# Seven half-width products in place of one 256-cubed product, in three steps of a PSUM bank, and four token sums moved to GpSimd

## The chip, the cores and the metric

The program runs on one core of a Trainium2 chip. The metric is the device time of one execution in microseconds (us). The kernel before took 820.01 us (median of 3 runs, 819.54 to 820.28).

## What is computed

4096 tokens of width 1024 are normalized. From the normalized tokens two branches start. One is a gate with a recurrence over the sequence; the other a feed-forward with three weight matrices, whose rows are then added into only eight rows of the output, because the top-2 expert indices (0 to 7) are used as row indices:

```python
g = sigmoid(einsum('btd,ed->bte', u, gate_w) + gate_b)
u_g = u * g
...
h = silu(xr @ w1.T)
h = silu(h @ w3.T)
h = h @ w2.T
...
out = out.at[indices_k[:, k]].add(gates[:, k:k + 1] * h)
...
x = x + s * silu(ffn)
```

So all tokens go through `w1` and `w3` (two 1024 x 1024 matrices, float32), only the first 1024 tokens through the gate matrix, and `w2` is applied after the sum over tokens, to eight rows.

## The kernel before

**Groups and halves.** The 4096 tokens are cut into four groups (`sb` 0 to 3) of 1024. For a group the product with `w1` is called `u`, with `w3` is called `m`, and with the gate matrix `g` (group 0 only). Each is a 1024-cubed product done by two levels of Strassen in Winograd's form. The first level leaves seven products of 512 cubed; one such product is one `Half` (L885), numbered `i` 1 to 7 and run in the order of L205. The second level leaves seven products of 256 cubed, one per step of a half (`step`, L919).

**One step.** `small` (L869) does a 256-cubed product with four matmuls of 128 weights columns and 256 moving columns. The profile has two rows for each float32 matmul, here called passes, so that a step is eight passes. A half keeps its sums in three PSUM banks: `X` (steps 0, 2, 4, 6), `Z` (steps 1, 5) and `Y` (step 3 alone). After each step the bank, as it then stands, is added on VectorE to a quarter of the half's result in SBUF (`first`, L904, and `more`, L912; for halves 1 and 5, which have nothing to add to, `first` is a copy on ScalarE). There are two `X` banks, two `Z` banks and one `Y` bank (L104 to L106).

**Order.** Every engine's instructions run in the order in which the program emits them (`Pinned`, L79). The emission follows "places": a half starts 7 places after the one before and does step n at its start S + 2n, so two halves interleave and one place is one step of TensorE. Around the end of a half (place S + 12) TensorE's order is: step 6 of this half, step 3 of the next half, step 0 of the one after it, which takes over this half's `X` bank. Work for other engines is entered with `at(place, ...)` (L186) and emitted when the place comes.

**Operands.** The sums of tokens within a half (`left_sums`, L846) are four GpSimd subtractions or additions of 128 x 512 into "quarters", tiles of 128 x 512 in SBUF; there are 18 (L125). They are emitted 8 places ahead of their step. The sums of tokens for the first level (`s1` to `s4`, L785 to L844, four 128 x 512 instructions each) run on the engine that `s_engine` (L779) names: GpSimd for `u` of groups 1 to 3, VectorE for `m`. In group 0 the weights' sums are made and kept in DRAM; groups 1 to 3 load them again with `load_kept` and `load_kept_sum` (L629, L635), issued on SyncE's queue 9 or 10 places ahead.

**What comes between.** In `m` of groups 1 and 2 the tokens of the next group are normalized (`norm`, L407) with VectorE instructions of 128 x 1024, one every 1.9 places. Halves 6 and 7 add two blocks on VectorE after each quarter (`whole`, L1005). The routing of a group (`route`, L439) is spread over the first halves of its `u`; its one-hot sums on VectorE wait for two sigmoids on ScalarE.

Of the kernel before, what the change touches and what calls it, by code (L numbers as in the profile page):

```python
# [10 lines left out]
F32 = mybir.dt.float32  # L11
# [3 lines left out]
ALU = mybir.AluOpType  # L15
AX = mybir.AxisListType
P = 128
Q = 256
# [4 lines left out]
def kernel(  # L23
# [55 lines left out]
    class Pinned:  # L79
# [15 lines left out]
    nc = tc.nc  # L95
    pe, dve, act, pool, sync = (
        Pinned(e) for e in (nc.tensor, nc.vector, nc.scalar, nc.gpsimd, nc.sync)
    )
# [7 lines left out]
    ps_y = ctx.enter_context(tc.tile_pool(name="ps_y", bufs=1, space=bass.MemoryType.PSUM))  # L106
# [15 lines left out]
            if self.uses == 0:  # L122
                self.home.append(self.tile)

    NB, NQ = 20, 18  # L125
    IDLE = 13
    blocks = deque(
        const.tile([P, 4, 2 * Q], F32, tag=f"b{i}", name=f"b{i}") for i in range(NB)
# [8 lines left out]
    def quarter(uses=1):  # L137
        return Held(quarters, uses)
# [47 lines left out]
    def at(place, f, *args):  # L186

        seq[0] += 1
        heapq.heappush(todo, (place, seq[0], f, args))
# [8 lines left out]
    def resume(p, g):  # L198
        step = next(g, None)
        if step is not None:  # L200
            at(p + step, resume, p + step, g)
# [14 lines left out]
    start = {}  # L216
# [301 lines left out]
    kept = {}  # L518
    op_t = {}
# [14 lines left out]
    def keep_quarter(name, i, j, o):  # L534
        d = dramp.tile([P, 2 * Q], F32, tag=f"{name}_{i}_{j}", name=f"{name}_{i}_{j}")
        sync.dma_start(d, o.tile)
        kept[name, i, j] = d
        o.drop()
# [177 lines left out]
    def first_w3():  # L716
# [48 lines left out]
    S_OF = {  # L765
        1: (0, 0),
        2: (0, 1),
        4: (1, 1),
        5: "s1",
        6: "s2",  # L770
        3: "s4",
        7: "s3",
    }
    left = {}
# [2 lines left out]
    A_AT = (1, 2, 4, 5)  # L777

    def s_engine(kind, sb):  # L779
        return pool if kind == "u" and sb > 0 else dve  # L780


    BANKS = {("u", 0): (0, 1), ("m", 0): (0,)}
# [1 line left out]
    def s1(kind, sb, n):  # L785
        eng = s_engine(kind, sb)
        a21, a22 = left[kind, sb, (1, 0)], left[kind, sb, (1, 1)]
        o = block(1 + n)
        if (kind, sb) in BANKS:
            yield from with_bank(o, a21, a22, (3, 0, 1, 2), op=ALU.add, of=BANKS[kind, sb])  # L790
        else:
            for q in (3, 0, 1, 2):
                eng.tensor_tensor(o[:, q], a21[:, q], a22[:, q], ALU.add)
                if q == 0:
                    yield 0.5
        a21.drop()
        a22.drop()
        left[kind, sb, "s1"] = o

    def s2(kind, sb, n):  # L800
        eng = s_engine(kind, sb)
        while (kind, sb, "s1") not in left:
            yield 0.25
        p, a11 = left[kind, sb, "s1"], left[kind, sb, (0, 0)]
        o = block(2 * n)
        if (kind, sb) in BANKS:
            yield from with_bank(o, p, a11, (2, 3, 0, 1), of=BANKS[kind, sb])
        else:
            for q in (2, 3, 0, 1):
                eng.tensor_tensor(o[:, q], p[:, q], a11[:, q], ALU.subtract)  # L810
                if q == 3:
                    yield 0.5
        p.drop()
        a11.drop()
        left[kind, sb, "s2"] = o

    def s4(kind, sb, n):

        eng = s_engine(kind, sb)
        while (kind, sb, "s2") not in left:  # L820
            yield 0.25
        o, a12 = left[kind, sb, "s2"], left[kind, sb, (0, 1)]
        if (kind, sb) == ("m", 0):
            yield from with_bank(o, o, a12, (2, 3, 0, 1), True, of=(0, 2))
        else:
            for q in (2, 3, 0, 1):
                eng.tensor_tensor(o[:, q], a12[:, q], o[:, q], ALU.subtract)
                yield 0.5
        a12.drop()
        left[kind, sb, "s4"] = o  # L830
# [35 lines left out]
                yield 2 * (A_AT[j + 1] - A_AT[j])  # L866


    def small(ps, A, B, start, stop, rows_first):  # L869

        for mt in range(2):
            for kt in range(2):
                w, m = (A, B) if rows_first else (B, A)
                pe.matmul(
                    ps[:, mt * Q : (mt + 1) * Q],
                    w[:, kt * Q + mt * P : kt * Q + (mt + 1) * P],
                    m[:, kt * Q : (kt + 1) * Q],
                    start=(start and mt == 0 and kt == 0),
                    stop=(stop and mt == 1 and kt == 1),
                    skip_group_check=True,  # L880
                )
# [3 lines left out]
    class Half:  # L885
# [30 lines left out]
        def whole(self, q):  # L916
            whole(self.kind, self.sb, self.i, q)

        def step(self, n):  # L919
            if n == 0:  # L920
                self.begin()
            A, t = self.A, self.t
            ts = [op_ts.get((self.kind, self.sb, self.i, j)) for j in range(4)]
            s = [left_q.get((self.src, self.sb, self.i, j)) for j in range(4)]

            def go(ps, a, b, start, stop):
                small(ps, a, b, start, stop, self.rows_first)

            if self.plain:

                q = ((0, 1, 2, 3) if self.i == 1 else (0, 3, 1, 2))[n // 2]
                ps = self.X if n // 2 % 2 == 0 else self.Z
                go(ps, A[:, q // 2 * 2 + n % 2], t[:, n % 2 * 2 + q % 2], n % 2 == 0, n % 2 == 1)
                if n % 2:
                    self.first(q, ps)
            elif n == 0:
                go(self.X, A[:, 0], t[:, 0], True, False)
                self.first(0, self.X)
            elif n == 1:
                go(self.Z, s[0].tile, ts[0].tile, True, False)  # L940
                self.first(3, self.Z)
                s[0].drop()
                ts[0].drop()
            elif n == 2:
                go(self.X, s[1].tile, ts[1].tile, False, False)
                self.first(1, self.X)
                s[1].drop()
                ts[1].drop()
            elif n == 3:
                Y = ps_y.tile([P, 2 * Q], F32, tag="Y", name=f"Y_{self.tag}")  # L950
                go(Y, A[:, 1], t[:, 2], True, True)
                if (self.kind, self.i) == ("g", 1):
                    at(Y_AT, self.more, 0, Y)
                else:
                    self.more(0, Y)
            elif n == 4:
                go(self.X, s[2].tile, ts[2].tile, False, False)
                self.more(3, self.X)
                s[2].drop()
                ts[2].drop()  # L960
            elif n == 5:
                go(self.Z, s[3].tile, t[:, 3], False, True)
                self.more(1, self.Z)
                s[3].drop()
            elif n == 6:
                go(self.X, A[:, 3], ts[3].tile, False, True)
                self.first(2, self.X)
                self.whole(2)
                ts[3].drop()
            if n == (7 if self.plain else 6):  # L970
                self.A.drop()
                t.drop()
# [265 lines left out]
    for kind, sb, i, plain in line:  # L1238
        h = Half(kind, sb, i, plain)
        halves.append(h)  # L1240
        S = start[kind, sb, i]
        n = 2 if sb == 0 and kind == "u" and i not in PLAIN_G else 1
        if kind != "g" and not plain:
            at(S + 2 - 8, left_sums, kind, sb, i, n)
        if kind != "g" and sb > 0:
            at(S - 10, load_kept, kind, sb, i)
            for j in range(4):
                at(S + 2 * T_AT[j] - 9, load_kept_sum, kind, sb, i, j)

    for sb in range(NS):  # L1250
        n = 2 if sb == 0 else 1
# [252 lines left out]
```

## Time and profile before

| | us |
|---|---|
| median of the runs | 820.01 |
| profiled execution: first to last instruction (span) | 817.9 |
| TensorE matmul busy in it | 810.6 (99%), 4085 passes |
| VectorE busy | 509.7 (62%) |
| GpSimd busy | 496.1 (61%) |
| ScalarE busy | 263.8 (32%) |
| granted TensorE clock | 1.000 |
| one half of groups 1 to 3 on TensorE | 12.09 |

The profiled execution has no time of its own listed apart from its span; the median of the runs lies 2.1 us above the span, which is what surrounds the first and last instruction. In the rows of the timeline a line is: start in us, duration in us, engine, source line, operation, output<-inputs by tile names (buffer numbers left out), shape, number of instructions, and in brackets how long the engine had been idle and what released it. PE is TensorE's matmuls, PEld its weight loads, DVE VectorE, ACT ScalarE, POOL GpSimd, SP SyncE. A row with x8 is eight instructions in a row; its duration is from the first one's start to the last one's end, and a pass has an end that lies beyond the start of the next, since passes are pipelined. All compute rows have line L89, the helper that records them, so groups are told apart by tiles: `b` are the 128 x 2048 blocks, `q` the quarters, `X_m`, `Y_u` and so on the PSUM banks of a half, `bc` the rows of means and scales for the normalization.

The busy share of each engine by stretch of groups 1 to 3 (`u` and `m` of each group) is:

| stretch, us | what | VectorE busy, us | GpSimd busy, us |
|---|---|---|---|
| 292.2 to 358.5 | most of group 1's `u` | 35.12 of 66.3 | 39.92 |
| 358.5 to 469.0 | group 1's `m`, start of group 2's `u` | 70.03 of 110.5 | 60.32 |
| 469.0 to 535.3 | group 2's `u` | 35.09 of 66.3 | 34.79 |
| 535.3 to 645.8 | group 2's `m`, start of group 3's `u` | 70.04 of 110.5 | 60.31 |

### The profile page before, as it was taken

Reading aid. Unit: us, or ns where it says so; the run is one execution under the profiler, and the core shown is the slowest. Engines: PE = TensorE matmul, PEld = TensorE weight load, DVE = VectorE, ACT = ScalarE, POOL = GpSimd, SP = SyncE. Lnnn points to the kernel's source line nnn. Section 1 sums busy time; section 2 is a strip of 40 time slices with the busy share of each in tenths; the row PEclk is TensorE's granted clock in tenths of the full one; section 3 lists DMA queues with packets and bytes.
Section 4 is the critical chain, followed back from the end, with each engine's and each line's share of the span. In section 5 each row is a group of like instructions: output and inputs, shape, how many; then the busy total and the mean of one; then the engine's idle time right before and its main releaser. Section 6 shows DMA issues by size and latency. Waiting matters only on the chain.

```text
span 817.9 us, 11299 instructions
## 1 busy us (share of the span) xinstructions
PE 810.6 (99%) x4085; PEld 696.5 (85%) x4085; DVE 509.7 (62%) x868; ACT 263.8 (32%) x458; POOL 496.1 (61%) x398
## 2 busy tenths in 40 slices
PE   8999999999999999999999999999999999999997
PEld 7888888888888878888888788888888788888885
DVE  6886598765588524764985235666983246667643
ACT  1245126877232237341022065421122021220111
POOL 2799896967999394744547453755448454465300
PEclk9999999999999999999999999999999999999999
DMA  9946619465978947629955875559666365555700
GB/s 338 421 175 232 230 47 357 171 246 160 411 267 309 345 174 293 241 103 385 376 179 210 332 279 190 187 206 426 242 244 257 104 219 203 196 180 195 283 14 2
DMA packets 55927, 192.88 MB, mean 236 GB/s; under 512 B 6480, under 2 KB 9792, under 8 KB 44224
## 3 DMA queue, kind: packets, MB, share of 16 engines
q1 hardware_dynamic: 55552, 191.61, 63.5%
q8 instruction: 33, 0.54, 0.3%
q10 hardware_dynamic: 320, 0.54, 0.2%
q14 instruction: 22, 0.18, 0.1%
HBM read 169.01 MB, written 39.87 MB: 255 GB/s over the span
## 4 chain that ended last, share of the span: by engine, by line
PE 98%; DMA 1%; DVE 0%; ACT 0%; issue 0%; SPq 0%
PE X_u L89 24%; PE X_m L89 24%; PE Z_u L89 12%; PE Z_m L89 12%; PE X_g L89 6%; PE Y_m L89 6%; PE Y_u L89 6%; PE Z_g L89 3%; PE acc L89 2%; PE plT L89 2%; PE Y_g L89 1%; DMA b<-in_x 1%; PE pp L89 0%; DVE bn L89 0%; PE accB L89 0%; PE ta L89 0%
## 5 line engine op out<-in xcount | busy, mean ns | idle before, releaser
L89 POOL TENSOR_TENSOR q<-b 128x512 f32<-128x512 f32 x154 | 203.0, 1331 | 193.7 <-PE X_m L89 48.0
L89 ACT ACTIVATE b<-b 128x512 f32<-128x512 f32 (+1 forms) x152 | 105.3, 696 | 298.1 <-DVE b L89 291.6
L89 POOL TENSOR_TENSOR q<-b,q 128x512 f32<-128x512 f32 x98 | 133.1, 1361 | 7.2 <-issue 4.0
L89 POOL TENSOR_TENSOR b<-b,b 128x512 f32<-128x512 f32 x72 | 92.9, 1310 | 48.5 <-PE X_u L89 33.7
L89 DVE TENSOR_TENSOR b<-b,b 128x512 f32<-128x512 f32 x120 | 109.2, 925 | 2.7
L89 PE MATMUL X_m<-q,q 128*128 128x256 f32 x448 | 105.9, 379 | 0.0
L89 PE MATMUL X_u<-q,q 128*128 128x256 f32 x432 | 102.4, 380 | 0.0
L89 DVE TENSOR_TENSOR b<-X_u,b 128x512 f32<-128x512 f32 x87 | 60.0, 690 | 57.8 <-PE X_u L89 57.1
L89 DVE TENSOR_TENSOR b<-X_m,b 128x512 f32<-128x512 f32 x88 | 60.4, 688 | 56.9 <-PE X_m L89 56.7
L89 PEld LDWEIGHTS X_m<-q,q 128*128 128x128 f32 x448 | 85.0, 190 | 12.4 <-issue 0.8
L89 POOL TENSOR_TENSOR q<-q,b 128x512 f32<-128x512 f32 x56 | 73.6, 1314 | 32.4 <-PE X_u L89 25.1
L89 PEld LDWEIGHTS X_u<-q,q 128*128 128x128 f32 x432 | 81.8, 190 | 12.2 <-issue 1.2
L89 DVE TENSOR_TENSOR b<-b,bc 128x1024 f32<-128x1024 f32 x56 | 67.8, 1211 | 0.1
L89 PE MATMUL X_u<-b,b 128*128 128x256 f32 x248 | 58.4, 380 | 0.0
L89 PE MATMUL Y_m<-b,b 128*128 128x256 f32 x224 | 53.1, 380 | 0.0
L89 PE MATMUL Z_m<-b,q 128*128 128x256 f32 x224 | 53.0, 380 | 0.0
L89 PE MATMUL X_m<-b,b 128*128 128x256 f32 x224 | 53.0, 379 | 0.0
L89 PE MATMUL Z_m<-q,q 128*128 128x256 f32 x224 | 52.9, 379 | 0.0
L89 PE MATMUL X_m<-q,b 128*128 128x256 f32 x224 | 52.9, 379 | 0.0
L89 PEld LDWEIGHTS X_u<-b,b 128*128 128x128 f32 x248 | 47.0, 190 | 6.7 <-DVE b L89 0.4
L89 DVE TENSOR_TENSOR b<-Z_u,b 128x512 f32<-128x512 f32 x47 | 32.4, 690 | 31.6 <-PE Z_u L89 30.7
L89 PE MATMUL Z_u<-q,q 128*128 128x256 f32 x216 | 51.1, 380 | 0.0
(182 smaller groups left out, 1171.6 us busy)
## 6 DMA issues: line engine op xcount, KB each, us to landing
q<-w SPq DMA_DIRECT2D x168, 256.0 KB, 4.5
b<-in_w SPq DMA_DIRECT2D x36, 1024.0 KB, 9.0
b<-w_T SPq DMA_DIRECT2D x24, 1024.0 KB, 6.3
b<-in_xT SPq DMA_DIRECT2D x15, 1024.0 KB, 12.9
w<-q SPq DMA_DIRECT2D x56, 256.0 KB, 7.4
b<-in_x SPq DMA_DIRECT2D x12, 1024.0 KB, 11.0
w_T<-b SPq DMA_DIRECT2D x8, 1024.0 KB, 4.4
b<-in_gw SPq DMA_DIRECT2D x6, 1024.0 KB, 14.0
```

Of the source, the lines that this page charges most:

```text
L89: r = f(*args, **kwargs)
```

## The change

Step 3 of the halves `u` and `m` of groups 1 to 3 (42 halves) is replaced: its product of 256 cubed is done by a third level of Strassen, seven products of 128 cubed (one matmul each, 128 weights columns and 128 moving columns) in the four 128-column parts of the half's `Y` bank. They run in three steps of that bank: `eighth(0)` (two matmuls) just before place S + 1, `eighth(1)` (one matmul) at S + 3.6, `eighth(2)` (four matmuls) in the place of step 3, at S + 6. After each step VectorE adds parts of the bank to parts of the result's quarter 0: two additions of 128 x 128, then one, then one of 128 x 512 and one of 128 x 128.

The operands need sums of 128 x 128 parts. Those of the tokens (`token_thirds`) are three GpSimd instructions for each half (one writes two parts), at places S - 2 and S - 1. Those of the weights are made in group 1 by four GpSimd instructions for each half (`weight_thirds`, S - 3 to S - 1) and written to DRAM; groups 2 and 3 load them (`load_thirds`, S - 3). Six more quarters hold them; the space comes from a smaller scratch for dynamic DMAs.

`s_engine` gives GpSimd also to `m` of groups 1 to 3: 16 instructions of 128 x 512 for each group move from VectorE to GpSimd.

```diff
-    NB, NQ = 20, 18
+    NB, NQ = 20, 24
...
     def s_engine(kind, sb):
-        return pool if kind == "u" and sb > 0 else dve
+        return pool if sb > 0 else dve
...
+    def token_thirds(kind, sb, i):
+        a = cut(left[kind, sb, S_OF[i]][:, 1])
+        t = quarter()
+        o = cut(t.tile)
+        third_s[kind, sb, i] = t
+        pool.tensor_tensor(
+            o[:, 0:2], a[:, 1:2].to_broadcast([P, 2, P]), a[:, 0::3], ALU.subtract
+        )
+        yield 1
+        pool.tensor_tensor(o[:, 2], a[:, 0], o[:, 1], ALU.subtract)
+        pool.tensor_tensor(o[:, 3], a[:, 2], o[:, 2], ALU.subtract)
+
+    def weight_thirds(kind, sb, i):
+        name = {"u": "w1", "m": "w3"}[kind]
+        b = cut(op_t[kind, sb, i][:, 2])
+        t = quarter(2)
+        o = cut(t.tile)
+        third_t[kind, sb, i] = t
+        pool.tensor_tensor(o[:, 1], b[:, 1], b[:, 0], ALU.subtract)
+        yield 1
+        pool.tensor_tensor(o[:, 2], b[:, 3], o[:, 1], ALU.add)
+        pool.tensor_tensor(o[:, 3], b[:, 2], o[:, 2], ALU.subtract)
+        yield 1
+        pool.tensor_tensor(o[:, 0], b[:, 1], b[:, 3], ALU.add)
+        yield 1
+        keep_quarter(name, i, "t", t)
+
+    def load_thirds(kind, sb, i):
+        o = quarter()
+        sync.dma_start(o.tile, kept[{"u": "w1", "m": "w3"}[kind], i, "t"])
+        third_t[kind, sb, i] = o
...
+        def eighth(self, n):
+            key = self.kind, self.sb, self.i
+            a, b = cut(self.A[:, 1]), cut(self.t[:, 2])
+            S, T = cut(third_s[key].tile), cut(third_t[key].tile)
+            d = cut(self.dst[:, 0])
+            z, w = (1, 2) if self.rows_first else (2, 1)
+            if n == 0:
+                self.Y = ps_y.tile([P, 2 * Q], F32, tag="Y", name=f"Y_{self.tag}")
+            ps = cut(self.Y)
...
+            if n == 0:
+                go(3, a[:, 0], b[:, 0], True, False)
+                go(z, S[:, 1], T[:, 1], False, False)
+                add(d[:, 0], ps[:, 3])
+                add(d[:, 3], ps[:, z])
+            elif n == 1:
+                go(3, S[:, 2], T[:, 2], False, False)
+                add(d[:, z], ps[:, 3])
+            else:
+                go(z, S[:, 3], b[:, 3], False, False)
+                go(w, a[:, 3], T[:, 3], False, False)
+                go(0, a[:, 2], b[:, 2], False, False)
+                go(3, S[:, 0], T[:, 0], False, True)
+                add(self.dst[:, 0], self.Y)
+                add(d[:, w], ps[:, 3])
+                third_s[key].drop()
+                third_t[key].drop()
+                self.whole(0)
...
+            elif n == 3 and is_third(self.kind, self.sb, self.i):
+                self.eighth(2)
...
+        if is_third(kind, sb, i):
+            for n, step in enumerate((1, 3.6)):
+                at(S + step, h.eighth, n)
+            at(S - 2, token_thirds, kind, sb, i)
+            at(S - 3, *((weight_thirds if sb == 1 else load_thirds), kind, sb, i))
...
-    nc = bacc.Bacc("TRN2", target_bir_lowering=False, num_devices=1)
+    nc = bacc.Bacc("TRN2", target_bir_lowering=False, num_devices=1, dynamic_dma_scratch_size=1024)
```

`cut` views a quarter as four parts of 128 columns; `go(o, p, q, ...)` is one matmul of parts p and q into part o of the bank; `add(o, p)` adds part p of the bank to o on VectorE.

More of the change, by code (lines that the diff above doesn't have):

```diff
@@ L866, in left_sums, with is_third, cut @@
                 yield 2 * (A_AT[j + 1] - A_AT[j])
+    third_s = {}
+    third_t = {}
+    def is_third(kind, sb, i):
+        return sb > 0 and kind != "g"
+    def cut(t):
+        return t.rearrange("p (k n) -> p k n", n=P)
+    def token_thirds(kind, sb, i):
[27 more added lines that the diff above has]
+        third_t[kind, sb, i] = o
     def small(ps, A, B, start, stop, rows_first):
@@ L917, in whole, with go, add @@
             whole(self.kind, self.sb, self.i, q)
+        def eighth(self, n):
[7 more added lines that the diff above has]
+            ps = cut(self.Y)
+            def go(o, p, q, start, stop):
+                left_side, right_side = (p, q) if self.rows_first else (q, p)
+                pe.matmul(
+                    ps[:, o], left_side, right_side, start=start, stop=stop, skip_group_check=True
+                )
+            def add(o, p):
+                dve.tensor_add(o, p, o)
+            if n == 0:
[16 more added lines that the diff above has]
+                self.whole(0)
         def step(self, n):
```

## Prediction

> **What bounds the kernel now.** I read the page's busy shares, then the chain that ended last, then the timeline of TensorE with its weight loads.
>
> ```profile
> PE 98%; DMA 1%; DVE 0%; ACT 0%; issue 0%; SPq 0%
> ```
>
> ```profile
> 8.75 0.83 PE L89 MATMUL idle<-ident,ones 128*128 128x128 f32 x6
> 9.62 3.72 PE L89 MATMUL X_u<-b,b 128*128 128x256 f32 x16
> 13.18 1.89 PE L89 MATMUL X_g<-b,b 128*128 128x256 f32 x8
> ```
>
> ```profile
> 811.73 0.61 PE L89 MATMUL ta<-sel,b 128*128 128x8 f32 x4
> ```
>
> TensorE is the chain, at full clock, with almost no idle time: a half of groups 1 to 3 lasts 12.09 us, seven steps of 1.73. So time saved on TensorE is time saved, and any wait on TensorE is lost. A pass of 256 columns comes every (1.89 - 0.38) / 7 = 0.216 us, a pass of 128 columns every (0.83 - 0.275) / 5 = 0.111 (0.38 and 0.275 are the lengths of single rows). A pass of 8 columns (ta) comes every (0.61 - 0.26) / 3 = 0.116, no sooner: 128 columns already stand at the floor of load plus pass, so the short passes of the change will cost 0.1117 (the x4 row of the same warming matmuls gives that).
>
> **Term 1, the products.** Step 3 goes from 8 passes of 0.2158 (1.726 us) to 14 of 0.1117 (1.564). 42 halves x 0.163 = **-6.8 us**. [...]
>
> **Term 2, the X bank.** What follows step 3 matters more. TensorE runs step 6 of a half, step 3 of the next, then step 0 of the one after, which needs the first half's X bank. Its last reader is the addition (or ScalarE copy) after step 6. Step 3 covers that: 1.73 us so far. In the change only `eighth(2)` stands there, 8 passes x 0.1117 = 0.89.
>
> ```profile
> 417.27 1.89 PE L89 MATMUL Y_m<-b,b 128*128 128x256 f32 x8
> 417.47 0.69 DVE L89 TENSOR_TENSOR b<-X_m,b 128x512 f32<-128x512 f32 x1 [1.03 <-PE X_m L89]
> 418.08 1.21 DVE L89 TENSOR_TENSOR b<-b,bc 128x1024 f32<-128x1024 f32 x1
> ...
> 419.21 0.68 DVE L89 TENSOR_TENSOR b<-Y_m,b 128x512 f32<-128x512 f32 x1
> ```
>
> The X addition starts 0.20 after step 6 has ended and ends at 0.89. How a late release costs, one place shows already now, where a copy was late behind another:
>
> ```profile
> 393.07 1.89 PE L89 MATMUL Y_m<-b,b 128*128 128x256 f32 x8
> ...
> 393.56 0.59 ACT L89 COPY bc<-q 128x512 f32<-128x512 f32 x1 [11.79 <-DVE b L89]
> 394.09 0.58 ACT L89 COPY b<-X_m 128x512 f32<-128x512 f32 x1
> ...
> 394.72 1.38 PEld L89 LDWEIGHTS X_m<-b,b 128*128 128x128 f32 x7 [0.16 <-ACT b L89]
> 394.80 1.48 PE L89 MATMUL X_m<-b,b 128*128 128x256 f32 x6
> ```
>
> The weight load itself waits; it starts 0.05 after the copy's end (394.67). A load that is not hidden costs 0.10 more: the 16 passes at 9.62, which follow a wait, took 3.72 where 15 x 0.216 + 0.38 = 3.62. So the bank is usable 0.05 + 0.10 after its reader's end: at 1.05, due at 0.89. I expect 0.16 us of stall at each of 30 halves whose predecessor ends in a VectorE addition, 0.05 where it is a ScalarE copy of 0.585 (10 halves), and for the two late copies above (1.02 + 0.58 + 0.15 - 0.89) 0.86 each. Sum 4.8 + 0.5 + 1.7 = **+7.0 us**, which alone eats term 1.
>
> **Term 3, the Y bank.** There is one. Now it is filled at S + 6 and next at S + 13. After the change the next half's `eighth(0)` wants it at S + 8, after one step 0. Counted from the end of the predecessor's step 6, it is due at 0.89 + 0.16 + 1.73 = 2.78. With VectorE free, the addition of 512 starts 0.20 after `eighth(2)` at 1.09, takes 0.69, and the dependent one of 128 follows (0.03, as dependent rows do) with 0.30 (between the rows of 64 columns, 0.21, and of 256, 0.42). Free at 2.11 + 0.15 = 2.27: nothing lost. But VectorE works in order, and where other work stands before the Y addition it starts late. From its start, 0.69 + 0.03 + 0.30 + 0.15 = 1.17 remains:
> - Half 5 of `u`: the routing stands in front.
>
> ```profile
> 308.36 1.89 PE L89 MATMUL Y_u<-b,b 128*128 128x256 f32 x8
> ...
> 310.00 1.28 ACT L89 ACT_TABLE_LOAD   x1
> ...
> 311.30 0.39 ACT L89 ACTIVATE pl<-df 128x8 f32<-128x8 f32 x2
> ...
> 311.72 0.23 DVE L89 TENSOR_TENSOR oh<-pl,ix 128x64 f32<-128x64 f32 x1 [2.40 <-ACT pl L89]
> 311.86 0.68 DVE L89 TENSOR_TENSOR b<-Y_u,b 128x512 f32<-128x512 f32 x1
> ```
>
> The Y addition starts 3.50 after step 6 ended; 3.50 + 1.17 - 2.78 = 1.89. Three groups: 5.7. Today this lateness costs nothing.
> - Halves 4 and 2 of `m` in groups 1 and 2: X addition, a block addition of `whole` and a normalization (1.13 of VectorE's pace) come first; at half 4 of group 1 the Y addition starts at 432.02, 2.66 after step 6 (429.36). 2.66 + 1.17 - 2.78 = 1.05, and 0.3 more at half 2, where the block addition was slowed to 0.97. Four halves: 4.5.
> - Half 7 of `m` in groups 1 and 2 and half 1 of `u` in group 1: a normalization alone, 1.94 (the rows above): 0.33 each, 1.0.
> - Half 7 of `u`, behind a block addition: 0 to 0.3, taken 0.5 for three.
>
> Sum **+11.7 us**. The additions after `eighth(0)` and `eighth(1)` have three steps (5.2 us) and two (3.5) before the bank is written again; the worst Y lag in the trace, 3.4 at half 2 of `m`, contains the token sums that leave VectorE. I cost them at nothing; that cover gone, each would cost its lateness as above.
>
> **Term 4, GpSimd.** No row shows a GpSimd sum of 128 or 256 columns. Its 512 columns take 1.27 undisturbed and come every 1.23. From below 128 columns cost a quarter, 0.32; from above, if only the memset's slope (0.31 - 0.20 for 128 columns) came off, 0.95. I take 0.39 and, for 256, 0.68 (the tiny memset's 0.10 fixed, the rest by length): the nearest row is the operation itself. Token parts are then 1.46 a half, weight parts 1.57 in group 1, moved sums 16 x 1.23 = 20 a group. Group 1 is the tight one: 7 x (4.9 + 1.46 + 1.57) + 20 = 75 us for the 84.6 us of its `m`, but not evenly spread. Between the release of the last `u` token sum (332.77, a wait for TensorE) and the first small product of half 5 of `m` (372.4) there are 39.6 us; GpSimd has 3 sums of that kind (4.6), 12 token quarters (at 1.35, 16.2), the eight moved sums (9.8) and 9.1 of parts: 39.7. **+1 us** for being just late. In groups 2 and 3 the weight parts (4.7 of it) are missing and it is early. VectorE loses 16 x 0.93 a group and gains 14 x 4 x 0.3, both hidden except as in terms 2 and 3. At 0.32 the late microsecond goes; at 0.95 see below.
>
> **Term 5, the queues.** 14 stores and 28 loads of 256 KB are 11 MB on 193. In group 1 SyncE's queue stands at each store until GpSimd has made the parts, and behind it are the loads of the next halves; it runs 6 to 8 places ahead now, 1 to 3 at the start of `m`, and a load is issued 9 or 10 ahead. The new loads have 4 places (6.9 us) plus that lead, against 4.5 to land. I cost this at nothing, up to 4 if landings reach the 9 us of the busy stretch at the start of `m`. No DMA is issued by GpSimd, so the scratch costs nothing.
>
> **Sum.** -6.8 + 7.0 + 11.7 + 1.0 = +12.9: span 817.9 to 830.8. With the 2.1 us that the median lies above it, **832.9 us**.
>
> **Rivals.**
> - Only the arithmetic counts: releases are hidden, 820.0 - 6.8 = 813.2. For it speaks that TensorE almost never waits now; against it the 0.89 us window and the load that waits at 394.72. Chance 0.12.
> - The X bank costs its 7.0, but the Y lateness dissolves since VectorE has less to do in `m`: 820.2, within 0.2%. Against: the routing chain hangs on ScalarE, not on VectorE's load. 0.06.
> - Half of term 3: 822 to 826. 0.08.
> - GpSimd becomes the bound (my own side, further out): at 0.95 for 128 and 1.06 for 256 columns a half of group 1 needs 4.9 + 2.9 + 3.0 + 3.8 = 14.6 of 12.09; 14 x 2.5 = 35 us more, up to 868. It decides from 0.56 a small sum. Against: memsets of 128 columns take 0.20. 0.12.
> - The forecast, 826 to 840: 0.62.
>
> Faster is the first rival, the other side of my forecast: 0.12. The measurement can tell about 0.2% from no change. Same 0.06, slower 0.82. The range 819 to 848 leaves out the first rival and the top of the GpSimd case.
>
> **What would show it.** Term 1: `Y_u` and `Y_m` rows of 128 columns every 0.11. Term 2: weight loads of `X` at every half idle before them, released by VectorE's `X` addition, and steps 0 late by 0.16. Term 3: weight loads of `Y` released by VectorE, 1 to 2 us late after half 5 of `u` and halves 2 and 4 of `m`. Term 4: weight loads of `Y_m` in group 1 released by GpSimd; its small sums near 0.39. Wrong I would be if step 0 did not wait for the X addition, or if GpSimd's small sums cost near 0.9.

## The result, and the profile after

The changed kernel takes 840.74 us (median of 4 runs, 838.68 to 841.86), the kernel before 819.99 beside it (819.54 to 820.28): ratio 1.025, 95% interval [1.0236, 1.0265]. It is slower by 20.8 us; forecast were 12.9 more. The direction and the mechanism stand, the size of the Y bank's term does not. The profiled execution is the longest of the four; its span of 840.1 us is 22.2 more than before.

From the page of the changed kernel, the busy shares and the chain that ended last:

```profile
PE 814.6 (97%) x4337; PEld 700.7 (83%) x4337; DVE 521.7 (62%) x988; ACT 263.8 (31%) x458; POOL 642.0 (76%) x628
...
PE 82%; DVE 9%; DMA 7%; ACT 1%; issue 1%; SPq 0%; DVEq 0%
```

TensorE's share of the chain fell from 98% to 82%, and VectorE and a DMA took its place: TensorE now waits. Where it waits is read from its starts. A pass of 256 columns that is followed by the next one later than 0.2158 us (128 columns: 0.1117) has an excess. Without the warming passes (`idle`), the excesses of the whole trace sum to 32.0 us, 4.1 before. So 27.9 us of waits came in and 6.8 us of products went, 21.0 in all; 0.1 in the warming and 1.0 behind the last pass make up the rest of the 22.2. By place, in groups 1 to 3:

| place | predicted | measured | what the trace shows |
|---|---|---|---|
| products | -6.8 | -6.8 | 588 short passes, 0.1117 apart |
| X bank at step 0 | 7.0 | 6.2, of which 0.4 stood before | 0.16 where VectorE adds, 0.05 where ScalarE copies |
| Y bank, half 5 of `u` | 5.7 | 5.6 | 3 x (1.81 + 0.07) |
| Y bank, halves 4 and 2 of `m`, groups 1 and 2 | 4.5 | 6.0 | 1.24 to 1.66, and 0.07 each |
| Y bank, one normalization in front (3 places) | 1.0 | 1.2 | 3 x (0.315 + 0.07) |
| Y bank, half 7 of `u` | 0.5 | 1.3 | 3 x (0.36 + 0.07) |
| Y bank, half 4 of `u` in groups 2 and 3, half 5 of `m` in group 3 | 0 | 3.6 | 0.94, 0.94, 1.48, and 0.07 each |
| `eighth(2)` behind `eighth(1)`'s addition, half 2 of `m` in group 1 | 0 | 1.0 | 0.97 |
| GpSimd | 1 | 0.3 | 0.24 + 0.10 at half 5 of `m` in group 1 |
| the load of small weight sums | 0 | 1.9 | 1.86 at half 6 of `m` in group 2 |

The 0.07 is what the second pass after such a wait comes late. The rest of the 27.9, about 1 us, lies in group 0's start.

The answer to the rows of step 6, step 3 and step 0 shown of before, at one end of a half of `m` in group 1 (timeline, all engines):

```profile
424.63 0.69 DVE L89 TENSOR_TENSOR b<-X_m,b 128x512 f32<-128x512 f32 x1 [1.03 <-PE X_m L89]
...
425.09 0.39 PE L89 MATMUL Y_m<-q,q 128*128 128x128 f32 x2
425.23 1.21 DVE L89 TENSOR_TENSOR b<-b,bc 128x1024 f32<-128x1024 f32 x1
...
425.37 1.99 PE L89 MATMUL X_m<-b,b 128*128 128x256 f32 x8
426.36 1.01 DVE L89 TENSOR_TENSOR b<-Y_m,b 128x512 f32<-128x512 f32 x2
...
427.49 0.30 PEld L89 LDWEIGHTS Y_m<-b,b 128*128 128x128 f32 x2 [0.52 <-PE X_m L89]
427.52 0.46 PE L89 MATMUL Y_m<-b,b 128*128 128x128 f32 x2 [0.15 <-DVE b L89]
```

Both windows stand here. The last small product starts at 425.09 + 0.11; step 0 could follow at 425.31, but the X addition ends at 424.63 + 0.69 = 425.32, and step 0 starts 0.05 later; its eight passes take 1.99 in place of 1.89, which is the load that nothing hid. Then the Y additions (0.69 and 0.28, one row here) wait behind the X addition and a normalization, end at 427.37, and `eighth(0)` starts at 427.52 in place of 427.20. The releaser in the last PEld row, PE's X pass, is a guess of the profile; the row below names VectorE.

Half 5 of `u` in group 1, where the routing stands in front:

```profile
313.53 0.39 ACT L89 ACTIVATE pl<-df 128x8 f32<-128x8 f32 x2
...
313.95 0.23 DVE L89 TENSOR_TENSOR oh<-pl,ix 128x64 f32<-128x64 f32 x1 [2.40 <-ACT pl L89]
314.10 1.01 DVE L89 TENSOR_TENSOR b<-Y_u,b 128x512 f32<-128x512 f32 x2
...
315.25 0.46 PE L89 MATMUL Y_u<-b,b 128*128 128x128 f32 x2 [1.64 <-DVE oh L89]
```

VectorE stands idle for 2.40 us until the sigmoids, with the Y additions queued behind; they end at 315.11, and TensorE takes the bank 0.14 later.

### The profile page after: what moved, and what is told of

The parts are those of the page before. It is cut to its first block, busy times and chain, and to the rows that moved or that the text cites. A ratio compares the mean times of both kernels' runs of the same rounds, so it can differ in the third digit from the quotient of the medians.

```text
span 840.1 us, 12340 instructions
## 1 busy us (share of the span) xinstructions
PE 814.6 (97%) x4337; PEld 700.7 (83%) x4337; DVE 521.7 (62%) x988; ACT 263.8 (31%) x458; POOL 642.0 (76%) x628
## 4 chain that ended last, share of the span: by engine, by line
PE 82%; DVE 9%; DMA 7%; ACT 1%; issue 1%; SPq 0%; DVEq 0%
PE X_u L89 20%; PE X_m L89 18%; PE Z_u L89 11%; PE Z_m L89 10%; DVE b L89 8%; PE X_g L89 5%; PE Y_u L89 4%; PE Y_m L89 4%; PE Z_g L89 3%; PE acc L89 2%; PE plT L89 2%; DMA b<-in_x 2%; DMA b<-in_xT 2%; DMA q<-w 1%; DMA q<-w_t 1%; PE Y_g L89 1%
## 5 line engine op out<-in xcount | busy, mean ns | idle before, releaser
L89 POOL TENSOR_TENSOR q<-b 128x512 f32<-128x512 f32 (+2 forms) x224 | 244.6, 1108 | 64.8 <-DVE b L89 24.0
L89 POOL TENSOR_TENSOR b<-b,b 128x512 f32<-128x512 f32 x120 | 152.4, 1289 | 78.1 <-PE X_u L89 31.5
L89 POOL TENSOR_TENSOR q<-b,q 128x128 f32<-128x128 f32 (+1 forms) x210 | 183.4, 877 | 15.3 <-PE X_u L89 7.2
L89 PEld LDWEIGHTS X_m<-q,q 128*128 128x128 f32 x448 | 81.8, 190 | 10.2 <-issue 0.8
L89 PEld LDWEIGHTS X_u<-q,q 128*128 128x128 f32 x432 | 78.8, 190 | 10.2 <-issue 1.2
L89 DVE TENSOR_TENSOR b<-b,b 128x512 f32<-128x512 f32 x72 | 70.5, 983 | 3.0
L89 DVE TENSOR_TENSOR b<-Y_m,b 128x128 f32<-128x128 f32 (+1 forms) x112 | 41.4, 385 | 32.5 <-PE Y_m L89 23.7
L89 PE MATMUL X_u<-b,b 128*128 128x256 f32 x248 | 60.2, 386 | 0.4 <-DMA b<-in_w 0.3
L89 DVE TENSOR_TENSOR b<-Y_u,b 128x128 f32<-128x128 f32 (+1 forms) x111 | 40.7, 383 | 26.2 <-PE Y_u L89 17.8
L89 DVE TENSOR_TENSOR b<-Z_m,b 128x512 f32<-128x512 f32 x48 | 32.8, 688 | 32.1 <-PE Z_m L89 31.6
```

What stands on the lines that cost most here:

```text
L89: r = f(*args, **kwargs)
```

## The experiments

### The token sums of `m` back on VectorE

```diff
-        return pool if sb > 0 else dve
+        return pool if kind == "u" and sb > 0 else dve
```

> The change, but the token sums of m stay on VectorE. Theory (late releases of the X and Y banks): GpSimd was never the bound, so nothing large is won; the sums stand again before the Y additions of halves 6 and 2 of m, and their stalls grow (half 2: Y addition 2.7 us after its bank is full, so about 2.8 us of wait in place of 1.4). 838 to 844 us. Rival (GpSimd's added load is what costs): the 60 us of sums leave it and most of the loss goes, below 832 us.

Measured: 846.04 us (844.63 to 846.89), ratio 1.0326 [1.0309, 1.0343]. It is 5 us slower than the change with them on GpSimd. So the sums on GpSimd are not what costs; VectorE's queue is, and this loads it more (550.7 us busy against 521.7). The size was missed by 2 us: one X wait of 0.99 follows a Y wait of 1.27 within 2 us, and the passes behind them run at half pace (granted clock 0.60 from 412.6 to 414.2 and 0.72 from 414.2 to 418.0), which costs about 1.7 us.

### The token sums of `m` on GpSimd alone, in the kernel before

```diff
-        return pool if kind == "u" and sb > 0 else dve
+        return pool if sb > 0 else dve
```

> The kernel before with only the token sums of m moved to GpSimd, no third level. Theory: TensorE has 1.73 us of cover at each X bank and seven places at each Y bank, so nothing waits: 819 to 821 us. Rival (the moved sums come late or slow VectorE): 823 us or more, with weight loads of X_m or Z_m released by GpSimd.

Measured: 819.37 us (818.86 to 820.24), ratio 1.0001 [0.9991, 1.001]. This part of the change has no time of its own.

### Steps 5 and 6 exchanged

```diff
-            elif n == 5:
+            elif n == self.z_last:
...
-            elif n == 6:
+            elif n == 11 - self.z_last:
```

`z_last` is 6 for the halves with eighths but the last, so the X bank's last step is done two places earlier. This kernel leaves the order of the sums: the next half takes up quarter 1 before this half's last addition to it.

> The change with steps 5 and 6 of its halves exchanged (but for the last half), so that the X bank's last addition comes two places earlier and nothing waits for it. Theory: the idle time at steps 0 goes, 6.2 us by the trace of after (0.16 at most halves, 0.8 once), perhaps 1 to 3 of it given back as the next wait for the Y bank comes 0.16 sooner at some halves: 834 to 838 us. Rival (step 0 waits for something else, an operand or SyncE): no gain, 839 to 842.

Measured: 838.53 us (836.65 to 839.28), ratio 1.0238 [1.0221, 1.0255], a miss by half a microsecond, and a poor test, since the sums on VectorE are also in another order. The X waits went (6.2 to 0.6), but the Y waits grew (half 5 of `u` 1.96 in place of 1.81, half 7 of `u` in group 1 1.10 in place of 0.36).

### `eighth(0)` one place later

```diff
-            for n, step in enumerate((1, 3.6)):
+            for n, step in enumerate((2, 3.6)):
```

> The change with the first two small products one place later (S + 2 in place of S + 1), so that one more step of 1.73 us lies between the last reading of the Y bank and its next writing. Theory: of the waits for the Y bank, 18.8 us in the trace of after, only what exceeds 1.73 stays (0.1 us at three halves); X waits stay: 821 to 826 us. Rival (the loss is GpSimd's or the queue's load, not the place): 836 or more.

Measured: 821.56 us (819.79 to 822.3, 10 runs), ratio 1.0021 [1.0012, 1.0031]. One digit takes 19 us back. The Y bank has one step more, and the waits in front of `eighth(0)` fall from 16.6 us to 0.4 and the one in front of `eighth(2)` from 0.97 to 0.07. The load's wait falls too, from 1.86 to 0.71, and two new ones of 0.28 stand in front of `eighth(1)`. The X waits stay, 5.6 us, and the -6.8 of the products pays for them. In the timeline of this variant, at the end of a half of `m` in group 1, step 0 is late as before, and `eighth(0)` follows one step on without a wait:

```profile
419.13 0.39 PE L89 MATMUL Y_m<-q,q 128*128 128x128 f32 x2
...
419.42 1.99 PE L89 MATMUL X_m<-b,b 128*128 128x256 f32 x8
...
420.40 1.01 DVE L89 TENSOR_TENSOR b<-Y_m,b 128x512 f32<-128x512 f32 x2
...
422.76 0.41 PEld L89 LDWEIGHTS Y_m<-b,b 128*128 128x128 f32 x2
```

### `eighth(2)` exchanged with step 2

```diff
-            elif n == 2:
+            elif n == 2 and is_third(self.kind, self.sb, self.i):
+                self.eighth(2)
+            elif n == (3 if is_third(self.kind, self.sb, self.i) else 2):
...
-            for n, step in enumerate((1, 3.6)):
+            for n, step in enumerate((1, 2.6)):
```

> The change with its last small step, eighth(2), exchanged with step 2 in the 42 halves (eighth(2) at S + 4, the X step with the second sum at S + 6, eighth(1) at S + 2.6 in place of 3.6, eighth(0) stays at S + 1). Between step 6 of one half and step 0 of the one after the next stands a whole step of 1.73 us again, and the Y bank has four places until its next use in place of two. Theory (the price is the two windows, X about 6 and Y about 19 us, and neither the small products nor GpSimd's sums have a price of their own): both go, -6.8 of the products is left, with 1 to 4 us for the load of small weight sums that lands late in group 2 and for the additions after eighth(0) and eighth(1), which have one place less each: 814 to 818 us. Rival (VectorE and GpSimd together are late whatever the order): the waits move to eighth(1) and eighth(2), which have two steps and one step of time behind the step before them: 822 to 830.

Measured: 825.52 us (824.77 to 828.32), ratio 1.007 [1.0054, 1.0087]. The theory is wrong by 7.5 us, and the time lies in the rival's range. The two windows did open, but others closed. Where the rival had its waits, in front of `eighth(2)`, there are 1.9 us (1.02 and twice 0.42), released by VectorE. The rest it did not have: step 2's X bank is now taken up again by step 4 after one step only, and its copy on ScalarE stands behind the routing's table load (1.19 us in groups 1 and 2); additions of X in `m` are late by 0.1 to 0.95; the wait for the load of the small sums, in front of the second product of `eighth(0)` as in the change, is 2.36 in place of 1.86, and the passes behind it run at half pace (granted clock 0.62 from 567.5 to 572.0), about 1.7 us more.

### The same, with the small weight sums loaded earlier

```diff
-            at(S - 3, *((weight_thirds if sb == 1 else load_thirds), kind, sb, i))
+            at(S - (3 if sb == 1 else 8), *((weight_thirds if sb == 1 else load_thirds), kind, sb, i))
```

> The same exchange, and in groups 2 and 3 the load of the small weight sums issued at S - 8 in place of S - 3. Theory: the one wait for that load (1.86 us at half 6 of m in group 2 in the changed kernel) goes, 0.7 to 2 us below the exchange alone: 812.5 to 816. Rival (SyncE's queue is the limit, so an earlier load only makes another one late): no gain, or up to 2 us more than the exchange alone.

Measured: 823.4 us (823.05 to 823.94), ratio 1.0046 [1.0029, 1.0063]. The level was missed with the one above; the gain of 2.1 is at the theory's upper end. The half pace went with the load's wait (mean granted clock 0.998, where the exchange alone had 0.997).

### The change, with that load earlier

> The change as it is, with the load of the small weight sums in groups 2 and 3 issued at S - 8 in place of S - 3. Theory: the wait of 1.86 us at half 6 of m in group 2 was for this load alone and goes, nothing else moves: 838.0 to 839.5. Rival (SyncE's queue is full there): no gain, 840 to 842.

The edit is the one above, made to the change. Measured: 838.4 us (838.2 to 838.58), ratio 1.0231 [1.0214, 1.0248], 2.3 below the change. So the wait shown here, of the changed kernel's timeline, was for that load and its late issue:

```profile
572.76 0.38 PE L89 MATMUL Y_m<-b,b 128*128 128x128 f32 x2
574.84 0.46 PE L89 MATMUL Y_m<-q,q 128*128 128x128 f32 x2 [1.69 <-DMA q<-w_t]
```

### The small sums left out

```diff
-            S, T = cut(third_s[key].tile), cut(third_t[key].tile)
+            S, T = a, b
...
-            at(S - 2, token_thirds, kind, sb, i)
-            at(S - 3, *((weight_thirds if sb == 1 else load_thirds), kind, sb, i))
```

> The change without the sums of 128 x 128 parts: GpSimd makes none for tokens or weights, nothing is stored or loaded for them, and the small products take the plain parts in their place (so quarter 0 is another number; the products, the bank's steps and VectorE's additions stay). Theory: X waits stay at about 6 and the Y waits that stood in the prediction stay (half 5 of u 1.8 each, halves 4 and 2 of m in groups 1 and 2 from 1.0 to 1.4 each, normalizations 0.3 each); those that it did not have (half 4 of u in groups 2 and 3, 0.94 each, half 5 of m in group 3, 1.48) come from VectorE's additions slowed beside GpSimd's small sums and go, with the waits for the load (1.86) and for GpSimd (0.3): 832 to 836. Rival (the added waits come from VectorE's own five additions in place of one): only the 2.2 us of load and GpSimd go, 838 to 840.

Measured: 847.5 us (847.35 to 847.73), ratio 1.0343 [1.0325, 1.036]. Less work, and 7 us slower than the change; neither theory had that. The trace has one wait of 11.28 us on TensorE in `m` of group 3, and this in front of it (timeline, all engines; POOL is GpSimd):

```profile
744.25 2.52 POOL L89 TENSOR_TENSOR q<-b 128x512 f32<-128x512 f32 x2
744.58 14.45 DVE L89 TENSOR_TENSOR uv<-lrv_sb,rk 128x32 f32<-128x32 f32 x1
...
757.70 1.27 POOL L89 TENSOR_TENSOR q<-q,b 128x512 f32<-128x512 f32 x1
758.90 0.32 POOL L89 MEMSET b<- 128x256 f32 x1
759.06 0.19 DVE L89 TENSOR_REDUCE pd<-uv 128x8 f32<-128x32 f32 x1
```

An instruction of 128 x 32 that took 0.32 us in the changed kernel stands for 14.45 us, while GpSimd goes through twelve sums of 128 x 512 without a pause (one was running, eleven came after), and it ends as GpSimd's next instruction is a memset. That was a guess from one trace, so the next kernel tests it.

### The same, with gaps on GpSimd

```diff
+    gap = const.tile([P, 1], F32, tag="gap", name="gap")
+    for n in range(40):
+        at(start["m", NS - 1, 1] - 8 + 0.9 * n, pool.memset, gap, 0.0)
```

> The variant without the small sums (847.5 us), and in m of group 3 forty GpSimd memsets of one column into a tile that nobody reads, one every 0.9 places, between GpSimd's sums. In the variant without them one VectorE addition with both operands in SBUF (uv, 128 x 32) stood for 14.45 us, while GpSimd went through eleven sums of 128 x 512 without a pause, and it ended as a memset of GpSimd began. Theory (VectorE's instruction gets no turn between GpSimd's sums, but does beside an instruction that reads nothing): it takes under 3 us, the stall of 11.28 us on TensorE goes with the passes at half pace behind it, and what is left is the change without its small sums: 833 to 837 us. Rival (its length has another cause, such as the other numbers in the kernel): 846 to 848.

Measured: 835.69 us (834.5 to 836.86), ratio 1.0196 [1.018, 1.0211]. The same instruction, in this kernel's timeline:

```profile
744.89 0.85 DVE L89 TENSOR_TENSOR uv<-lrv_sb,rk 128x32 f32<-128x32 f32 x1
```

Forty instructions more and 11.8 us less: the theory holds. The memset at 758.90 agrees: it reads nothing, and the addition ended 0.13 us after it began (744.58 + 14.45 = 759.03). Why the addition stood through all twelve sums ahead of it, and not through one, no run shows.

This kernel also answers what the one before should have told. Against the change, 840.74 - 835.69 = 5.0 us is what the small sums cost with their stores and loads. In the traces the waits for the load (1.9) and for GpSimd (0.3) went, and the Y bank's waits on VectorE are 2.0 shorter. The waits at half 4 of `u` in groups 2 and 3 fell only from 0.94 to 0.70 and 0.76, and that at half 5 of `m` in group 3 from 1.48 to 0.88, where the forty memsets stand too; half 4 of `u` in group 1 even has 0.70 that it had not before. So most of those waits is not made by the small sums. The block addition in front of the Y additions is longer where a GpSimd sum of 128 x 512 is running, as the rows of half 4 of `u` below show.

### Step 6 one place earlier

```diff
-        (at_first[kind, sb, i][n] if (kind, sb, i) in at_first else start[kind, sb, i] + 2 * n, k, n)
+        (at_first[kind, sb, i][n] if (kind, sb, i) in at_first else start[kind, sb, i] + 2 * n - (1.1 if n == 6 and is_third(kind, sb, i) else 0), k, n)
```

> The change with step 6 of the 42 halves moved one place earlier, ahead of the next half's step 2 (place S + 10.9 in place of S + 12), and the load of its second operand one place earlier; the order in which the quarters are added up stays. Between step 6 and the step 0 that takes over its X bank there are now 1.73 + 0.89 us. Theory (the X waits are the short window alone): the 6.2 us of X waits go. The Y bank stays as late as before or becomes due 0.16 us earlier after each half, so the Y waits stay at 18 to 21: 834 to 838 us. Rival (all of term 2 is given back to the Y bank, since TensorE only arrives there earlier): 839 to 841.

Measured: 833.06 us (831.14 to 834.75), ratio 1.0162 [1.0144, 1.0179], 7.7 below the change and 0.9 under the expected span. The X waits went, from 6.2 us to 0.6. This is the fair test of the X bank that the exchange of steps 5 and 6 was not. But not all of the 7.7 is the X bank's: the Y waits (with that of `eighth(2)`) fell from 17.5 to 14.0, which neither theory had and no run explains, and a stretch at half clock, described below, took 1.5 to 1.7 back.

### Both windows, and the earlier load

The three edits, step 6 one place earlier, `eighth(0)` at S + 2 and the load at S - 8, together.

> Both windows at once: step 6 one place earlier as in the kernel above, eighth(0) at S + 2 in place of S + 1, and the load of the small weight sums issued at S - 8 in groups 2 and 3. Theory (the two banks' windows are the whole price, the load the only other wait): X waits 5.6 us and the load's 0.7 below the variant with eighth(0) at S + 2 alone (821.56), 814.5 to 817 us, faster than both kernels. Rival (X and Y exchange their waits, as they did when steps 5 and 6 were exchanged): 818.5 to 822.

Measured: 816.62 us (815.9 to 817.76, 5 runs), ratio 0.9963 [0.995, 0.9977]. It beats the kernel before by 0.37% and the change by 24 us, with the same products and the same sums. All excesses of its trace, counted as above, come to 7.8 us, 3.7 more than before, out of 6.8 that the products save. The largest of those left is 0.79 near the end, in front of the last small products (`pp`); step 6 moved alone has it too.

### The routing one place later

```diff
         pool.memset(c, 0.0)
+        yield 1 if sb else 0
```

> The change with the one-hot sums of the routing emitted one place later in groups 1 to 3, so that on VectorE the two Y additions of half 5 of u stand ahead of the first of them instead of behind it. Theory (the Y bank after half 5 of u is late only because VectorE's queue stands at that sum until ScalarE's sigmoids are done): the three waits of 1.81 us and the 0.07 behind each go, nothing comes in their place, since the X addition now behind the sum has two steps until its bank is needed: 840.7 - 5.6 = 835.1, 834 to 836.5 us. Rival (VectorE is late there as a whole, or ScalarE's sigmoids make the next additions late): the wait goes to the X bank or to eighth(1), 838 to 841.

Measured: 834.66 us (833.87 to 836.79), ratio 1.0187 [1.0169, 1.0206], 6.1 below the change. The rows that answer to those of the changed kernel above:

```profile
311.07 1.02 DVE L89 TENSOR_TENSOR b<-Y_u,b 128x512 f32<-128x512 f32 x2
...
312.83 0.38 PE L89 MATMUL Y_u<-b,b 128*128 128x128 f32 x2
...
313.34 0.23 DVE L89 TENSOR_TENSOR oh<-pl,ix 128x64 f32<-128x64 f32 x1 [1.25 <-ACT pl L89]
```

The Y additions run in the time in which VectorE stood idle for ScalarE, and `eighth(0)` does not wait. All three waits of 1.81 are gone from the trace and nothing took their place there. Elsewhere two waits changed: that for the load grew from 1.86 to 2.70, and that at half 5 of `m` in group 3 fell from 1.48 to 0.30.

## Why the prediction was right, and where its sum was short

The forecast's 826 to 840 us ends 0.7 below the 840.74 measured. The waits stand where terms 2 and 3 put them; the sum was 7.8 us short, most of it in term 3.

**Term 1, the products, held to the tenth.** The short passes came every 0.1117 us, as the warming matmuls had shown.

**Term 2, the X bank, held in its mechanism: +7.0 forecast, 5.8 measured.** 0.055 for the release and 0.104 for the load that nothing hides, where 0.16 was taken. The two late ScalarE copies (0.86 each) did not occur: the copy of rows and the X copy were 1.2 us apart. In group 1 the former stands 2.7 us later than before and TensorE 4.7, so the earlier waits had moved them against each other. One X wait of 0.81 in group 2, behind a late VectorE, was not forecast and makes up for one of the two by luck. Moving step 6 took 7.7 us off, 5.5 of it X waits.

**Term 3, the Y bank, had the right mechanism and was mis-sized: +11.7 forecast, 18.7 measured.** Moving `eighth(0)` alone took 19.2 us off, 1.2 of it from the wait for the load. Where the trace of before showed what stood in front of the Y addition the places were right: 1.88 against 1.89 at half 5 of `u`, and the routing experiment took these three off. What was short:
- The sum itself: two halves at 1.05 and two at 1.35 are 4.8, where 4.5 was entered.
- Halves 4 and 2 of `m` were worked out with block additions as long as before (0.66 to 0.97). They took up to 1.30, and half 4 of `u`, which was not on the list at all, has one of 1.74:

```profile
719.08 2.95 POOL L89 TENSOR_TENSOR q<-b 128x512 f32<-128x512 f32 x2
719.16 1.74 DVE L89 TENSOR_TENSOR b<-b,b 128x512 f32<-128x512 f32 x1
...
720.82 1.00 DVE L89 TENSOR_TENSOR b<-Y_u,b 128x512 f32<-128x512 f32 x2
...
721.97 0.46 PE L89 MATMUL Y_u<-b,b 128*128 128x128 f32 x2 [0.78 <-DVE b L89]
```

 Before, two such additions together took 1.28 there (group 2):

```profile
534.33 1.28 DVE L89 TENSOR_TENSOR b<-b,b 128x512 f32<-128x512 f32 x2
```

 The list counted instructions in front of the Y addition and not how long they take beside a GpSimd that is now busy for 76% of the span. The trace of before already had this price: in groups 1 to 3 it has 32 block additions of over 0.9 us, up to 1.80, and the changed kernel 19, and every one of them begins while a GpSimd sum is running. Of the 79 that took 0.75 or less in the two traces, 14 do.
- Half 5 of `m` in group 3 waits for the recurrence's scans, which also stand in front of a Y addition. The prediction listed the routing, and not this other chain of small VectorE instructions.
- "The additions after `eighth(0)` and `eighth(1)` have three steps and two: I cost them at nothing" was wrong at one place, by 1.0 us, behind two slowed block additions and two normalizations.

**Term 4, GpSimd, was close in its price and wrong in its place.** A sum of 128 columns takes 0.457 us (median), of 256 columns 0.728, where 0.39 and 0.68 were taken, under the 0.56 from which GpSimd would have become the bound. As a wait of TensorE on GpSimd it cost 0.3. But small sums left out are worth 5.0 us together with their load, 2.0 of it by way of VectorE.

**Term 5, the queues, costed at nothing, was 1.9 us** in the trace and 2.3 by experiment, within the 0 to 4 given.

Of the rivals, the one in which the Y lateness dissolves fell with the Y rows of the table; that the arithmetic alone counts fell with the X and Y rows, though the combination of both windows comes near to it: 816.6, where that rival said 813.2. GpSimd as the bound fell with the 0.457, and half of term 3 with the 18.7.

## What to carry to other kernels

The step in front of the X bank's next use was made shorter here, from 1.73 us to 0.89, and the release chain (reader's end, 0.05, an unhidden load of 0.10) was paid from half to half, 0.16 us where VectorE adds; the X waits came to 6.2 us in all. So look for the order that puts a full step there before counting the products saved: here two moves of one place and an earlier load made 24 us. And a low busy share does not say that an engine is in time: VectorE, 62% busy, stood idle for 2.40 us until the sigmoids, and the Y additions queued behind cost TensorE 1.81 us in each of three groups.

## What the runs showed of the hardware

- A VectorE addition of 128 x 32 with both operands in SBUF took 14.45 us beside a run of twelve GpSimd sums, 0.85 with memsets between them, and 0.32 in the changed kernel. By the same reading, shorter forms of it are the scans of the recurrence, two of which took 2.39 us in the changed kernel, and the block additions of 1.3 to 1.74. Additions of 128 x 512 that read PSUM kept their 0.69 throughout (0.67 to 0.69 in the changed kernel). It is not two operands alone: the recurrence's copy of 128 x 64, with one, took 1.13 us in the changed kernel and 0.18 in the variant without the small sums.
- In four of the profiled executions TensorE came back from a wait at about half the clock. In the variant with step 6 earlier, around a wait of 2.2 us in group 1 (stretches of the window table; the granted clock is the number after POOL's):

```profile
312.50:315.00 2.50, 0.44 (x3) 0.27 (x3) 1.50 (x5) 2.46 (x6) 2.50 (x3) 1.00 0.84 246
315.40:319.00 3.60, 3.60 (x12) 2.98 (x12) 0.60 (x4) 2.72 (x7) 3.52 (x7) 0.58 0.98 345
319.00:323.00 4.00, 4.00 (x21) 3.55 (x20) 2.26 (x6) 0.00 (x0) 3.92 (x6) 1.00 1.42 564
```

 Half is 0.50, as the changed kernel's window table has it from 837 to 840, behind its last pass. By the second row above the clock was at half for 0.42 x 3.60 / 0.5 = 3.0 us behind 315.40, and by the first not yet at 315.00: 3.0 to 3.4 us, an estimate from these two rows, which is another 1.5 to 1.7 us on top of the wait. The same arithmetic gives 3.4 us with the token sums back on VectorE (0.60 over 1.60 us and 0.72 over 3.80), behind waits of 1.27 and 0.99 close together; 3.4 with `eighth(2)` exchanged with step 2 (0.62 over 4.50), behind a wait of 2.36; and over 9 with the small sums left out (0.69 over 10.00 and 0.54 over 3.20), in and behind the wait of 11.28. A wait of 2.10 in group 2 of the variant with step 6 earlier did not do it, nor did the changed kernel's 1.86, nor even the 2.70 of the routing variant. So the length of a single wait does not decide it in these runs, and what does was not shown: the same wait can cost nothing more or 1.7 us more.
